# Results of seven items, added behind named steps of the eighth item's attention and experts

## The chip, the core and the metric

The kernel runs on one core of one Trainium2 chip, in one launch. The metric is device microseconds of that core. Three executions of the kernel before took 2759.94, 2760.19 and 2761.65 us; the median is 2760.19 us. The profiled execution of the same kernel took 2850.38 us, with a span of 2848.7 us from the first to the last instruction, so all times read from its trace are on a scale that is about 3% longer than the timed one.

## What is computed

The input is a batch of 8 items of 256 channels on a 32x32 grid, which is 1024 tokens of 256 features each, all in float32. An item passes two layers:

```python
# layer 0: 8 heads of 64, softmax over the queries' axis
qkv  = xt @ w_qkv + b_qkv
attn = softmax(einsum('bihd,bjhd->bijh', q, k) * SCALE, axis=1)
x    = einsum('bijh,bjhd->bihd', attn, v) @ w_out + b_out + xt
# layer 1: one attention without heads, then 8 experts of which each token uses 2
t = t + softmax((ln(t) @ W.T) @ ln(t).T) @ ln(t)
u = ln(t)
t = t + u + sum over the token's two best experts e of gate_e * (gelu(u @ w1[e] + b1[e]) @ w2[e] + b2[e])
```

Items don't depend on each other, except that the kernel treats the experts of seven of them together.

## The kernel before

**Stages.** A loop over the items b = 0 to 7 runs layer 0 (`layer0`) and, for the first seven, the attention of layer 1 (`attend`) and `dispatch`. The last function normalizes the tokens, finds each token's two experts and gates, and scatters the normalized rows into a DRAM tensor `rows`, one region for each expert, by 16 indirect DMAs on GpSimd's queue for an item (L631). It also keeps, for each item, the expert number `exp` and the row `row` of every token, and stores `sums` (the tokens plus their normalized form) in DRAM.

Item 7 is different. After its `layer0` comes `experts`, which handles the 7 x 1024 x 2 rows of the others in 63 blocks of 256 rows: for a block it fetches the weights of its expert and its rows by two indirect DMAs (L736, L745), transposes the rows (L754, copied out as `xb` on L756), multiplies twice (L764, L789), adds the bias on VectorE (L798, `yb`) and writes the result to the DRAM tensor `y` (L803). Then `attend` runs for item 7, and `dense`, in which every expert is applied to all 1024 tokens of item 7, in 16 steps of one expert and one half of the tokens (`hidden`, L938, and `collect`, L962 and L971).

**The plan.** `plan` turns the counts of rows for each expert into the numbers that the blocks need: `row_at` and `w_at` (which rows and which weights block b fetches), some 25 small VectorE instructions (L655 to L704), and then, for each of the seven items and both of a token's experts, `yat`, the place in `y` where the token's result lies: 14 times five instructions (L712 to L725), 70 in all.

**The others' results.** `Results` brings the results of the seven items together. It works in 14 portions, one for each half of an item. For a portion, `gather` issues 8 indirect DMAs on GpSimd's queue (L830), each of which fetches 128 rows of `y` into one eighth of a buffer `yk`; there are two such buffers, so two portions can be on their way. `step` takes one portion: if it is the first half of an item it loads `sums` into a buffer `o` (L852, SyncE's queue; two buffers, used in turn), then adds the 8 gathered pieces with their gates (L857, VectorE, eight instructions), lets the gather of the portion after next begin, and at the second half calls `store`: 16 transposes on TensorE (L877), two copies on ScalarE (L879) and two transfers to the output (L880).

**What sets the order.** The engines execute their own instructions in the order in which the scheduler of the language has put them. The scheduler lists instructions by the order in which the program makes them and by when it believes their inputs to be ready; it places instructions of one engine ahead of others when it expects a gap. The program says with `early` and `late` after which iterations of `attend` and of `dense` a portion is taken:

```python
        early = {3: 1, 4: 1, 5: 1, 6: 1, 7: 1}
        late = {0: 1, 1: 1, 2: 1, 4: 1, 5: 1, 7: 1, 8: 1, 10: 1, 12: 1}
```

Nothing keeps the scheduler from putting the additions of a portion ahead of that place. `tc.issue_after(instruction)`, which the kernel used before in `prepare`, does so: what the block under it makes on that instruction's engine is placed behind it. Instructions on other engines are not bound by it.

**Names along the way.** In `attend`, iteration i computes scores (L456, `ps`), their row maximum (VectorE, L464, `nmax`) and exponentials (ScalarE, L467, `ex`); `mix` then transposes them (L473, `pa`), copies them out (VectorE, L475, `aT`), multiplies by the tokens (L478, `py`) and adds the result (VectorE, L483). `mix` runs one iteration behind the scores. Before iteration 0 stand two copies of the projected tokens (VectorE, L448, `xa`). The PSUM pools have three buffers of two banks (`big`: scores, transposes, hidden layers, the output's transposes) and two of one bank (`acc`).

Of the kernel before, what the change touches and what calls it, by code (L numbers as in the profile page):

```python
# [18 lines left out]
def kernel(  # L19
# [23 lines left out]
    nc = tc.nc  # L43
    P = 128
    B, C, S = x.shape
# [6 lines left out]
    NH2 = S // 512  # L52
# [6 lines left out]
    NWB = 3  # L59
# [371 lines left out]
    def attend(b, t1, step=lambda i: None):  # L431
        n1 = one.tile([P, NT, D], F32, tag="n", name=f"n1_{b}")
        layer_norm(t1, n1, 1e-5, f"a{b}")
        nT = one.tile([P, NCC, S], F32, tag="nT", name=f"nT_{b}")
        to_channels(n1, nT, f"n1_{b}")
        xa = one.tile([P, NCC, S], F32, tag="xa", name=f"xa_{b}")
        for ec in range(NCC):
            px = big(f"px_{b}_{ec}")
            for dc in range(NCC):
                for n in range(NH2):  # L440
                    nc.tensor.matmul(
                        px[:, ts(n, 512)],
                        WT[:, dc, ts(ec, P)],
                        nT[:, dc, ts(n, 512)],
                        start=(dc == 0),
                        stop=(dc == NCC - 1),
                    )
            nc.vector.tensor_copy(xa[:, ec, :], px)  # L448

        t2 = t1  # L450

        def scores(i):
            psc = big(f"ps1_{b}_{i}")
            for ec in range(NCC):
                for n in range(NH2):
                    nc.tensor.matmul(  # L456
                        psc[:, ts(n, 512)],
                        xa[:, ec, ts(i, P)],
                        nT[:, ec, ts(n, 512)],
                        start=(ec == 0),  # L460
                        stop=(ec == NCC - 1),
                    )
            nmax = small.tile([P, 1], F32, tag="nmax", name=f"nmax_{b}_{i}")
            nc.vector.tensor_reduce(nmax, psc, AX.X, ALU.max, negate=True)  # L464
            ex = expp.tile([P, 1024], F32, tag="exps", name=f"ex1_{b}_{i}")
            ssum = small.tile([P, 1], F32, tag="ssum", name=f"ssum_{b}_{i}")
            nc.scalar.activation(ex, psc, AF.Exp, bias=nmax, scale=1.0, accum_out=ssum)  # L467
            return ex, ssum

        def mix(i, ex, ssum):  # L470
            pt = big(f"pa_{b}_{i}")
            for m in range(NT):
                nc.tensor.transpose(pt[:, ts(m, P)], ex[:, ts(m, P)], ident)  # L473
            aT = two.tile([P, S], F32, tag="tr", name=f"aT_{b}_{i}")
            nc.vector.tensor_copy(aT, pt)  # L475
            py = acc(f"py_{b}_{i}")
            for m in range(NT):
                nc.tensor.matmul(  # L478
                    py[:, :D], aT[:, ts(m, P)], n1[:, m, :], start=(m == 0), stop=(m == NT - 1)
                )  # L480
            rs = small.tile([P, 1], F32, tag="rs1", name=f"rs1_{b}_{i}")
            nc.vector.reciprocal(rs, ssum)
            nc.vector.scalar_tensor_tensor(  # L483
                t2[:, i, :], py[:, :D], rs, t1[:, i, :], ALU.mult, ALU.add
            )

        pending = None
        for i in range(NT):
            now = (i, *scores(i))
            if pending is not None:  # L490
                mix(*pending)
            pending = now
            step(i)
        mix(*pending)
        return t2

# [145 lines left out]
    def plan(group):  # L642


        n, nb, cap = group.n, group.nb, group.cap
        counts = group.counts
        steps = cap // BR
# [55 lines left out]
        w_at = keep.tile([P, NBMAX], I32, tag="w_at", name=f"w_at_{n}", bufs=2)  # L703
        nc.vector.tensor_copy(w_at[:, :nb], hi)  # L704


        for b in group.items:
            gate, kept = group.kept[b]
            ats = []
            for k, (row, exp) in enumerate(kept):  # L710
                hot = small.tile([P, NT, E], F32, tag="d_sel", name=f"p_hot_{b}_{k}", bufs=1)
                nc.vector.tensor_tensor(  # L712
                    hot,
                    exp.unsqueeze(2).to_broadcast([P, NT, E]),
                    e_iota.unsqueeze(1).to_broadcast([P, NT, E]),
                    ALU.is_equal,
                )
                nc.vector.tensor_mul(
                    hot, hot, first.unsqueeze(1).to_broadcast([P, NT, E])
                )  # L720
                to = small.tile([P, NT], F32, tag="d_to", name=f"p_to_{b}_{k}", bufs=2)
                nc.vector.tensor_reduce(to, hot, AX.X, ALU.add)
                nc.vector.scalar_tensor_tensor(to, to, float(BR), row, ALU.mult, ALU.add)
                at = keep.tile([P, NT], I32, tag=f"yat{k}", name=f"yat{k}_{b}")
                nc.vector.tensor_copy(at, to)  # L725
                ats.append(at)
            group.kept[b] = gate, ats
        return row_at, w_at

    def experts(group):  # L730
        n = group.n
# [51 lines left out]
        def collect(b, hT):  # L783
            wb = wbs[b % NWB]
            py = acc(f"pe_{n}_{b}")
            at = NCC * FF
            for r in range(R):
                for fc in range(NFC):
                    nc.tensor.matmul(  # L789
                        py[:, ts(r, D)],  # L790
                        hT[:, fc, ts(r, P)],
                        wb[:, at + fc * D : at + (fc + 1) * D],
                        start=(fc == 0),
                        stop=(fc == NFC - 1),
                    )
            at += NFC * D + NFC
            yb = two.tile([P, R, D], F32, tag="yb", name=f"yb_{n}_{b}")
            nc.vector.tensor_add(  # L798
                yb,
                py.rearrange("p (r d) -> p r d", d=D),  # L800
                wb[:, at : at + D].unsqueeze(1).to_broadcast([P, R, D]),
            )
            nc.sync.dma_start(group.y[ts(b, BR), :].rearrange("(p r) d -> p r d", r=R), yb)  # L803

        line = [None, None]
        for b in range(group.nb + 2):
# [77 lines left out]
    def dense(b, t2, step):  # L884
# [71 lines left out]
        def collect(e, n, hT):  # L956
            wb = wbs[e % NWB]
            for i in range(0, NT // NH2, 2):
                py = acc(f"pdy_{e}_{n}_{i}")
                for j in range(2):  # L960
                    for fc in range(NFC):
                        nc.tensor.matmul(  # L962
                            py[:, ts(j, D)],
                            hT[:, fc, ts(i + j, P)],
                            wb[:, NCC * FF + fc * D : NCC * FF + (fc + 1) * D],
                            start=(fc == 0),
                            stop=(fc == NFC - 1),
                        )
                for j in range(2):
                    block = n * (NT // NH2) + i + j  # L970
                    nc.vector.scalar_tensor_tensor(  # L971
                        t2[:, block, :],
                        py[:, ts(j, D)],
                        all_gates[:, block, e : e + 1],
                        t2[:, block, :],
                        ALU.mult,
                        ALU.add,
                    )
            if n == NH2 - 1 and e + NWB < E:
                weights(e + NWB)  # L980
            if e == E - 1:
                store(b, t2, range(n * (NT // NH2), (n + 1) * (NT // NH2)))

        pending = None
        for at, (e, n) in enumerate((e, n) for e in range(E) for n in range(NH2)):
            now = (e, n, hidden(e, n))
            if at == 1:
                biases()
            if pending is not None:
                collect(*pending)  # L990
            pending = now
            step(at)
        collect(*pending)

    for b in range(B):
        xT = next_x
        if b + 1 < B:
            next_x = load_x(b + 1)
        t1 = layer0(b, xT)
        if b + 1 < B:  # L1000
            t2 = attend(b, t1)
            dispatch(b, t2, groups[0])
            continue
        experts(groups[0])
        others = Results(groups[0])
        others.begin()

        early = {3: 1, 4: 1, 5: 1, 6: 1, 7: 1}
        late = {0: 1, 1: 1, 2: 1, 4: 1, 5: 1, 7: 1, 8: 1, 10: 1, 12: 1}

        def step(where, at):
            for _ in range(where.get(at, 0)):
                others.step()

        t2 = attend(b, t1, lambda i: step(early, i))
        dense(b, t2, lambda i: step(late, i))
        assert others.done == len(others.portions)
# [42 lines left out]
```

## Time and profile before

| | |
|---|---|
| timed, median of 3 | 2760.19 us |
| profiled execution, span | 2848.7 us |
| TensorE busy | 2656.4 us, 93% of the span |
| VectorE busy | 1540.0 us, 54% |
| ScalarE busy | 841.6 us, 30% |
| GpSimd busy | 384.9 us, 14% |
| mean granted TensorE clock | 0.964 |
| additions of the others' results (L857) | 112 x 479 ns (median) |
| gathers of results (L830) | 112 x 953 ns (median) |
| attention and experts of item 7 | 2543 to 2849 us of the span |

TensorE sets the pace over most of the span: in the layer 0 of an item it is busy without pause. Idle time on the other engines costs nothing there. It is different at the end, from 2543 us on, where the table of engines by stage (in the prediction below) shows TensorE idle for a third of the attention of item 7. The duration of an L830 row is [...]not the time until the rows have landed. The name in brackets behind an instruction of the timeline is what ended its engine's idle time before it; "issue" and "remote" mean that the profile shows no wait of the program that would explain it.

### The profile page before, as it was taken

The numbers are of one execution on the slowest core, as the hardware profiler recorded it, in microseconds if no ns is written. First come the engines' busy times: TensorE is split into PE (matmuls) and PEld (weight loads), VectorE is DVE, ScalarE is ACT, GpSimd is POOL, SyncE is SP. The second block draws the span as 40 slices with busy tenths as digits, with TensorE's granted clock in tenths as the row PEclk, the third lists the DMA queues.
The fourth block names the chain that finished last, engine by engine and source line by source line (L and its number), as shares of the span: only waits on it lengthen the run. The fifth ranks groups of instructions, "written<-read, shape, count | busy, mean of one in ns | idle before, by whom it ended". The sixth has DMA issues, their size and how long they took to land. (4 is left out here: it accounts for less than half of the span.)

```text
span 2848.7 us, 27710 instructions
## 1 busy us (share of the span) xinstructions
PE 2656.4 (93%) x10153; PEld 1401.7 (49%) x10153; DVE 1540.0 (54%) x3667; ACT 841.6 (30%) x1455; POOL 384.9 (14%) x383
## 2 busy tenths in 40 slices
PE   8999899989998999999999999999989999986789
PEld 3346434643365336533553356335633577764556
DVE  4664566456645674467456755565476633333442
ACT  2541154114511451045214521342125411111122
POOL 0000200020002000100011000200030044445540
PEclk9999999999999999999999999999989999997789
DMA  6981100010001000000000000000020155542351
GB/s 243 385 316 25 59 1 1 15 45 1 1 15 43 3 1 15 30 15 1 15 21 24 1 15 15 30 1 1 15 69 1 37 178 177 177 151 81 108 173 56
DMA packets 82512, 182.37 MB, mean 64 GB/s; under 512 B 15016, under 2 KB 24904, under 8 KB 80584
## 3 DMA queue, kind: packets, MB, share of 16 engines
q1 hardware_dynamic: 57368, 118.65, 11.6%
q0 software_dynamic: 25008, 61.95, 6.8%
q8 instruction: 80, 1.31, 0.2%
q14 instruction: 56, 0.46, 0.0%
HBM read 100.49 MB, written 110.90 MB: 74 GB/s over the span
## 5 line engine op out<-in xcount | busy, mean ns | idle before, releaser
L357 ACT ACTIVATE ex<-psc,nmax 128x1024 f32<-128x1024 f32 x512 | 565.8, 1109 | 827.6 <-DVE scrap L347 636.7
L324 PE MATMUL psc<-qk,qk 64*128 64x512 f32 x2048 | 590.7, 625 | 33.1 <-ACT ex L357 17.1
L382 PE MATMUL po<-ex,vs 128*64 128x512 f32 x2048 | 506.4, 616 | 8.1 <-DVE vs L366 7.1
L335 DVE TENSOR_REDUCE nmax<-psc 128x1 f32<-128x512 f32 x512 | 351.4, 687 | 169.4 <-PE psc L324 160.4
L324 PEld LDWEIGHTS psc<-qk,qk 64*128 64x128 f32 x2048 | 232.1, 186 | 385.7 <-ACT ex L357 187.3
L347 DVE TENSOR_SCALAR_CACHE_REDUCE scrap<-psc,nmax 128x512 f32<-128x512 f32 x512 | 382.2, 746 | 54.3 <-PE psc L324 22.5
L382 PEld LDWEIGHTS po<-ex,vs 128*64 128x64 f32 x2048 | 126.4, 137 | 352.6 <-issue 193.5
L478 PE MATMUL py<-n,aT 128*128 128x256 f32 x1024 | 243.3, 392 | 41.4 <-issue 21.9
L638 POOL TENSOR_TENSOR t<-t,n 128x2048 f32<-128x2048 f32 x7 | 31.6, 4512 | 1793.5 <-issue 1503.9
L456 PE MATMUL ps<-nT,xa 128*128 128x512 f32 x512 | 240.7, 600 | 10.6 <-DVE xa L448 5.7
L478 PEld LDWEIGHTS py<-n,aT 128*128 128x128 f32 x1024 | 195.6, 195 | 99.9 <-DVE aT L475 51.6
L273 PE MATMUL pqk<-xT,wqkv 128*128 128x512 f32 x512 | 238.7, 612 | 2.4 <-ACT ex L357 2.0
L281 DVE TENSOR_SCALAR qk<-pqk,b_qk 128x1024 f32<-128x1024 f32 x64 | 82.1, 1284 | 189.9 <-PE pqk L273 188.0
L467 ACT ACTIVATE ex<-ps,nmax 128x1024 f32<-128x1024 f32 x64 | 71.3, 1114 | 382.5 <-DVE nmax L464 359.8
L273 PEld LDWEIGHTS pqk<-xT,wqkv 128*128 128x128 f32 x512 | 95.7, 195 | 150.4 <-issue 104.7
L483 DVE SCALAR_TENSOR_TENSOR t<-py,rs,t 128x256 f32<-128x256 f32 x64 | 31.0, 484 | 242.8 <-PE py L478 215.5
L292 PE MATMUL pv<-wqkv,xT 128*128 128x512 f32 x256 | 138.5, 691 | 9.1 <-ACT wqkv L97 7.3
L456 PEld LDWEIGHTS ps<-nT,xa 128*128 128x128 f32 x512 | 94.7, 193 | 92.1 <-issue 79.9
L789 PE MATMUL pe<-wb,hb 128*128 128x256 f32 x504 | 125.5, 392 | 10.9 <-ACT hb L774 7.9
L631 POOL DMA_INDIRECT rows<-n,d_at x112 | 108.9, 973 | 158.6 <-DVE row L618 106.8
L830 POOL DMA_INDIRECT yk<-y,yat x112 | 111.9, 999 | 120.6 <-DVE o L857 71.5
L420 PE MATMUL pr<-wo,res 128*128 128x256 f32 x512 | 122.0, 381 | 0.0
(171 smaller groups left out, 2500.9 us busy)
## 6 DMA issues: line engine op xcount, KB each, us to landing
rows<-wb SPq DMA_DIRECT2D x7, 8192.0 KB
y<-yb SPq DMA_DIRECT2D x63, 256.0 KB
xT<-in_x_dram SPq DMA_DIRECT2D x7, 1024.0 KB
sums<-t SPq DMA_DIRECT2D x7, 1024.0 KB
o<-sums SPq DMA_DIRECT2D x7, 1024.0 KB
out_dram<-oT SPq DMA_DIRECT2D x14, 512.0 KB
wpack<-in_L_ffn_w_dram SPq DMA_DIRECT2D x4, 1024.0 KB
wb<-in_L_ffn_w_dram SPq DMA_DIRECT2D x16, 256.0 KB
```

What stands on the lines that cost most here:

```text
L273: nc.tensor.matmul(pq[:, ts(n, 512)], wqkv[:, cc, t, ts(g, P)], xT[:, cc, ts(n, 512)], start=(cc == 0), stop=(cc == NCC - 1),)
L292: nc.tensor.matmul(pv[:, ts(j, 512)], xT[:, cc, ts(i + j, P)], wqkv[:, cc, 2, :], start=(cc == 0), stop=(cc == NCC - 1),)
L324: mm = nc.tensor.matmul(pss[at, h][:, ts(n, 512)], k[r, ts(j, P)], q[r, ts(n, 512)], start=True, stop=True)
L335: firsts[at, h] = nc.vector.tensor_reduce(nmax, pss[at, h][:, ts(0, 512)], AX.X, ALU.max, negate=True)
L347: nc.vector.tensor_scalar(scrap, ps[:, ts(1, 512)], -1.0, nmaxes.pop((at, h)), ALU.mult, ALU.min, accum_out=nmax,)
L357: nc.scalar.activation(ex, ps, AF.Exp, bias=nmax, scale=1.0, accum_out=sums[at][:, h : h + 1])
L382: nc.tensor.matmul(po[n][h * DK : (h + 1) * DK, :], vs[:, h, :], exs[h][:, ts(n, 512)], start=(j == 0), stop=(j == NT - 1),)
L420: nc.tensor.matmul(pr[:, :C], res[:, g, ts(i, P)], wo[:, g, :], start=(g == 0), stop=False)
L456: nc.tensor.matmul(psc[:, ts(n, 512)], xa[:, ec, ts(i, P)], nT[:, ec, ts(n, 512)], start=(ec == 0), stop=(ec == NCC - 1),)
L478: nc.tensor.matmul(py[:, :D], aT[:, ts(m, P)], n1[:, m, :], start=(m == 0), stop=(m == NT - 1))
L789: nc.tensor.matmul(py[:, ts(r, D)], hT[:, fc, ts(r, P)], wb[:, at + fc * D : at + (fc + 1) * D], start=(fc == 0), stop=(fc == NFC - 1),)
L830: nc.gpsimd.indirect_dma_start(out=yk[:, i, k, :], out_offset=None, in_=self.group.y[:, :], in_offset=bass.IndirectOffsetOnAxis(ap=ats[k][ ...
```

## The change

Four edits, all of them in the order of instructions; the work is the same.

- The portions are bound to named instructions. In `attend`, `step(i)` moves from the loop into `mix`, behind the addition of iteration i (L483). In `dense`, it moves into `collect`, behind the last addition of that step (L971). The additions of a portion can no longer stand ahead of these on VectorE.
- `early` and `late` are set anew: six portions in the attention instead of five, two at once behind the first step of `dense`.
- The plan of the blocks is bound to the last copy of q and k of item 7's layer 0 (`evicted[7, 3, 1]`, L281), where before it could stand as soon as the counts were known.
- The places of results (`yat`) are taken out of the plan into a function `places`, bound to the bias addition of expert block 3 (L798).

Line numbers below are those of the kernel before; in the changed kernel the same lines stand 1 to 13 lines further down.

```diff
-            nc.vector.scalar_tensor_tensor(
+            mixed = nc.vector.scalar_tensor_tensor(
                 t2[:, i, :], py[:, :D], rs, t1[:, i, :], ALU.mult, ALU.add
             )
+            with tc.issue_after(mixed.ins):
+                step(i)
 ...
             pending = now
-            step(i)
         mix(*pending)
 ...
     def plan(group):
+        with tc.issue_after(evicted[B - 1, NPAIR - 1, 1].ins):
+            return plan_blocks(group)
+
+    def plan_blocks(group):
 ...
-
+        group.first = first
+        return row_at, w_at
+
+    def places(group):
+
+        first = group.first
         for b in group.items:
 ...
             group.kept[b] = gate, ats
-        return row_at, w_at
 ...
             nc.sync.dma_start(group.y[ts(b, BR), :].rearrange("(p r) d -> p r d", r=R), yb)
+            if b == NWB:
+                with tc.issue_after(added.ins):
+                    places(group)
 ...
+            with tc.issue_after(added.ins):
+                step(e * NH2 + n)
             if n == NH2 - 1 and e + NWB < E:
                 weights(e + NWB)
 ...
             pending = now
-            step(at)
         collect(*pending)
 ...
-        early = {3: 1, 4: 1, 5: 1, 6: 1, 7: 1}
-        late = {0: 1, 1: 1, 2: 1, 4: 1, 5: 1, 7: 1, 8: 1, 10: 1, 12: 1}
+        early = {1: 1, 2: 1, 3: 1, 5: 1, 6: 1, 7: 1}
+        late = {0: 2, 3: 1, 4: 1, 6: 1, 8: 1, 9: 1, 11: 1}
```

## The prediction, made before the changed kernel ran

> **What bounds the kernel now.** I read the page first: TensorE is busy 93% of the span and every other engine at most 54%, so other engines matter only where TensorE waits for them. The slices of the page show two such places: the end (from 2543 us), and a dip near 2100 us. Then I asked for the stages. The columns are: stretch and its length, busy us (and instructions) of PE, PEld, DVE, ACT and POOL, granted TensorE clock, DMA share, GB/s.
>
> ```profile
> 2543.20:2683.00 139.80, 89.53 (x329) 58.25 (x327) 60.32 (x121) 17.83 (x26) 76.08 (x78) 0.84 0.36 110
> ...
> 2690.00:2849.00 159.00, 144.28 (x536) 98.16 (x535) 54.51 (x141) 34.31 (x49) 33.92 (x33) 0.90 0.31 103
> ...
> 1206.79:1242.28 35.49, 31.69 (x96) 11.20 (x96) 19.77 (x46) 12.81 (x22) 9.94 (x11) 0.95 0.12 41
> 1787.38:1825.76 38.38, 33.09 (x96) 11.51 (x96) 19.75 (x46) 12.81 (x22) 9.92 (x11) 0.91 0.11 38
> 2083.92:2130.33 46.41, 35.96 (x97) 12.40 (x96) 29.23 (x117) 12.81 (x22) 16.64 (x17) 0.82 0.27 94
> ```
>
> The first two are item 7's attention and its experts. TensorE is idle for 50.3 of 139.8 us in the attention, and the clock falls to 0.84. The last three are the same work (from the first q and k of an item to those of its second pair of heads) at the start of items 4, 6 and 7: 35.5 us usually, 46.4 us in item 7, where VectorE has 9.5 us more to do, the plan.
>
> Then the timeline of item 7's attention, VectorE first:
>
> ```profile
> 2551.63 1.23 DVE L448 COPY xa<-px 128x1024 f32<-128x1024 f32 x1 [2.66 <-PE px L441]
> 2553.13 0.49 DVE L857 SCALAR_TENSOR_TENSOR o<-yk,gate,o 128x256 f32<-128x256 f32 x1 [0.27 <-DMA yk<-y,yat]
> ...
> 2560.73 0.48 DVE L857 SCALAR_TENSOR_TENSOR o<-yk,gate,o 128x256 f32<-128x256 f32 x1 [2.10 <-DMA yk<-y,yat]
> 2561.13 1.22 DVE L448 COPY xa<-px 128x1024 f32<-128x1024 f32 x1
> ...
> 2582.56 1.23 DVE L475 COPY aT<-pa 128x1024 f32<-128x1024 f32 x1 [4.65 <-remote]
> ...
> 2606.43 0.48 DVE L483 SCALAR_TENSOR_TENSOR t<-py,rs,t 128x256 f32<-128x256 f32 x1 [17.08 <-remote]
> ...
> 2668.60 0.48 DVE L483 SCALAR_TENSOR_TENSOR t<-py,rs,t 128x256 f32<-128x256 f32 x1 [5.99 <-remote]
> ```
>
> and what TensorE makes of it:
>
> ```profile
> 2562.40 8.36 PE L456 MATMUL ps<-nT,xa 128*128 128x512 f32 x12 [5.66 <-DVE xa L448]
> ...
> 2583.84 6.17 PE L478 MATMUL py<-n,aT 128*128 128x256 f32 x16 [10.49 <-issue]
> ...
> 2610.74 6.37 PE L478 MATMUL py<-n,aT 128*128 128x256 f32 x16 [9.69 <-DVE aT L475]
> ...
> 2620.42 3.72 PE L478 MATMUL py<-n,aT 128*128 128x256 f32 x16
> ```
>
> The second `xa` copy has its input at 2555.0 but stands behind five additions (L857), which wait for gathers, so it starts at 2561.1 and TensorE loses 5.66 us. The same happens to `aT` of iterations 0 and 1. Each pause also costs clock: the same 16 records take 6.2 to 6.4 us after one and 3.72 us without. In the experts the chain of waits names another wait, the load of `sums`, issued too late on SyncE's queue:
>
> ```profile
> 2706.12 6.44 DMA o<-sums
> ...
> 2738.89 5.97 DMA o<-sums
> ...
> 2759.28 6.55 DMA o<-sums
> ```
>
> At full clock the attention needs 74.6 us of TensorE: 2.0 + 7.1 (first transposes, projection), 8 x (3.44 + 0.87 + 3.45), two items' output transposes at 1.75. So 65 us are lost, 50 idle and 15 to the clock.
>
> **What I can't read.** The rows marked "remote" (4.65, 17.08, 5.99, and 3.35 before another `aT`; in the experts 1.34 and 4.97) are waits whose release the trace doesn't show. The inputs were there by the trace, and GpSimd had been issuing gathers without pause. The profiled execution is 90 us longer than the timed one (2850.38 against 2760.19). I take these pauses to belong to the profiled execution. Taking them out shifts the attention by 15 us at `aT` of iteration 1 and 12 us at the end, 27 together, and the experts by 8.7 (6.7 and 2 of clock). That leaves, as an estimate for the timed run, 113 us for the attention and 150 for the experts.
>
> **What the Trainium skill says.** "TensorE: Matmul & The Clock Gate", section "What's actually happening": after an idle window of about 3.4 us the array runs at half clock until it has been busy for about as long. The trace agrees (6.17 against 3.72 us above). "DMA: Bandwidth & Descriptors", section on one DMA on the gpsimd path: about 2.0 us plus bytes over 436 GB/s, 2.3 us for a gather of 128 KB. Here the first gather was issued at 2550.32 and its addition began at 2553.13, 2.8 us, the issue included. [...] "SBUF — State Buffer", section "Who interferes with whom": an operation with two SBUF inputs disturbs only GpSimd operations that read SBUF. The gathers keep their pace of 1.26 us (0.95 + 0.30) beside the additions, so I price that interference at nothing.
>
> **The change, part by part.**
>
> *Attention.* It takes away every addition ahead of `xa`, `nmax` and `aT` of iterations 0 and 1, and puts 8 (0.40 us start to start, 3.3 us) behind L483 of iterations 1, 2, 3, 5, 6, 7. Queued behind them are the next `nmax` and `aT`; ScalarE waits for the first, TensorE for both. Walking through with the durations above: `xa` ready at 2556.3, scores 0 and 1 done at 2561.6, `aT` 0 at 2564.3, `py` 0 done at 2567.9, `py` 1 at 2575.7. Then the additions show: the output's transposes stand on TensorE ahead of `py` 2 and wait for the first portion (1.3 us), `py` 2 waits for `aT` 2 (1.8 us), `aT` 7 stands behind the additions of iteration 6 (about 4.5 us), and small waits for PSUM buffers. I get L483 of iteration 7 at 2635.6. The last portion (3.3 us) lies on the path to the normalization: its transposes then start at 2640.8. Before, they start at 2683.05, without the unread pauses at 2656. Gain **15 us**. Are the gathers there in time? A portion is 8 x 1.26 = 10.1 us of GpSimd. Portions 0 and 1 end at 2570; portion 2 starts when the first is consumed (2579.5) and is needed at 2598.6; portion 3 is there at 2602, needed at 2614; 4 at 2614, needed at 2627; 5 at 2630, needed at 2636. Yes.
>
> *Experts.* The loads of `sums` now stand ahead of the item's output in SyncE's queue, and their buffers are free 20 us or more before use; so the three waits above go, and with them TensorE pauses of 1.9 and 2.4 us and about 3.5 us of clock behind the first. One portion less is left (0.9 us of transposes). Against this, the transposes of a portion wait in order for its additions, about 1.5 us at the two portions behind step 0. Gain **5 us**.
>
> *Start of item 7.* Plan and places leave 2075 to 2121 us. Of 46.41 - 35.48 = 10.9 us, item 6 shows 2.9 without any plan; of the other 8 about 2 go with a "remote" 2.70 us. Gain **6 us**.
>
> *Plan late in layer 0.* Its 25 instructions make about 6.6 us, spread over five steps of 3.9 us in which VectorE waits 0.6 to 1.0 us for TensorE. Five steps give about 4 us, the rest is exposed: **cost 3 us** (0 if the lag of two steps hides it, 6.6 if nothing does). It ends near 2230; the first block begins at 2272, so its fetches (1 us of issue each) are hidden.
>
> *Places among the expert blocks.* 70 instructions of about 0.17 us, 12 us, over eight half blocks with 1.47 us of idle VectorE each, 11.8 us. `xb` is needed 1.3 us after it is made, so the small overhang is hidden: **0** (4 at most).
>
> Sum: 15 + 5 + 6 - 3 - 0 = 23 us, 2760 - 23 = **2737 us**.
>
> **The rivals.**
> - *The unread pauses are in the timed run too* (20%). Then the old attention loses all 65 us. The new one has no more than 16 gathers in a row where the old had 40; if two thirds of 36 us go as well, 24 more: 2713. For it: the pauses come with long rows of gathers. Against: TensorE pauses too, without a wait of its own, and the total is long by 90 us in the profile.
> - *Smaller* (15%). In-order transposes and PSUM buffers (three, of which two now hold an output) eat the attention's gain down to 8, the start gives 5, the plan costs 3: 2750.
> - *Nothing* (7%): 8 more us lost in the same places, 2758.
> - *Slower* (6%). Every portion in the attention costs its 3.3 us and clock on top (30 of the 38 us that I think are lost now, a gain of 8), the eight in the experts cost 1.5 us each (-12, +7), plan 6.6 and places 6 are exposed, and the start gives 2: 2760 + 8 = 2768. Against it: four of the six are beside scores.
>
> **Numbers.** My case has 52%. The range is 2712 to 2754: below it lies half of the first rival, above it the last two. Faster by over 0.2% (below 2754.7): 0.52 + 0.20 + 0.15 = 0.87; within: 0.07; slower: 0.06.
>
> **What would show it.** In the profile of the changed kernel: both `xa` copies side by side and the first scores before 2560; no L857 wait on `sums`; attention near 98 us instead of 139.8; the start of item 7 at 36 to 40 us; the late part of layer 0 longer by up to 3 us; expert blocks still 4.33 us apart. I am wrong if TensorE's pauses only move: if it waits for the output's transposes behind additions in most iterations, if the plan stops layer 0 for more than 6 us, or if the gap between profiled and timed run stays at 90 us, which would mean that the pauses weren't the profiler's.

## The result: 12.7 us less, and the profile after

The changed kernel takes 2747.36 us (median of four executions, 2742.55 to 2748.91), the kernel before 2760.07 in the same comparison. The ratio is 0.9954, with a 95% interval of 0.9936 to 0.9972. The forecast was 23 us, 0.9917.

Not every run had the same chip: the kernel before takes 2759 to 2760 us beside this result and the runs e1 to e4, but 2857 to 2860 us on the three chips of e5 to e12, so a time is to be compared only with the kernel before beside it. I call them the first and the second kind of chip.

The profiled execution of before that the prediction reads took 2850.38 us, and fits the second kind. Its times aren't the timed ones on a longer scale: against e1 it is 45 us longer ahead of item 7's attention, 29 us in it and 16 us behind. Its stages are therefore no measure of the 12.7 us. I profiled the kernel before once more (e1, span 2758.1 us), and use that one here. The page of the changed kernel, and that of e1:

```profile
span 2745.2 us, 27697 instructions
...
PE 2617.9 (95%) x10153; PEld 1378.9 (50%) x10153; DVE 1539.6 (56%) x3667; ACT 841.2 (31%) x1455; POOL 385.7 (14%) x383
```

```profile
span 2758.1 us, 27710 instructions
...
PE 2620.8 (95%) x10153; PEld 1380.4 (50%) x10153; DVE 1544.5 (56%) x3667; ACT 842.3 (31%) x1455; POOL 386.8 (14%) x383
```

The work is the same; TensorE waits less. The engines by stage show where (columns as in the prediction). Kernel before, e1: attention of item 7, its experts, the start of item 7, the late part of its layer 0 (from its last q and k to the end of its output products):

```profile
2497.85:2608.80 110.95, 85.42 (x330) 56.20 (x328) 60.58 (x121) 18.09 (x26) 68.02 (x69) 0.92 0.43 130
2608.80:2758.10 149.30, 142.82 (x552) 96.41 (x552) 63.41 (x149) 34.62 (x50) 49.08 (x44) 0.93 0.38 120
2051.14:2084.95 33.81, 29.64 (x97) 10.51 (x96) 28.81 (x117) 12.82 (x22) 16.86 (x17) 1.00 0.38 129
2163.97:2226.66 62.69, 62.36 (x277) 30.72 (x277) 41.08 (x107) 27.64 (x47) 0.95 (x1) 1.00 0.06 22
```

Changed kernel, the same four stretches:

```profile
2496.84:2600.84 104.00, 87.86 (x346) 57.44 (x344) 52.70 (x105) 19.64 (x28) 57.42 (x60) 0.93 0.42 131
2600.84:2745.20 144.36, 138.16 (x536) 92.75 (x536) 64.82 (x165) 32.58 (x48) 59.68 (x54) 0.95 0.39 129
2051.03:2081.86 30.83, 29.00 (x96) 10.53 (x96) 19.76 (x46) 12.81 (x22) 9.94 (x11) 1.00 0.14 47
2160.86:2225.72 64.86, 62.56 (x276) 30.84 (x277) 45.73 (x127) 27.62 (x47) 6.95 (x7) 1.00 0.19 63
```

Attention -7.0 us, experts -4.9, start -3.0, plan +2.2: together -12.7 us. The 63 expert blocks take 270.9 us in both (first L764 or L773 to the attention's first transposes). VectorE's own load shows the moved plan: 28.81 to 19.76 us in the start, 41.08 to 45.73 in the late part.

The front of the attention is where the change does most. Kernel before, e1: VectorE's timeline, then TensorE's:

```profile
2506.27 1.22 DVE L448 COPY xa<-px 128x1024 f32<-128x1024 f32 x1 [2.66 <-PE px L441]
2507.84 0.48 DVE L857 SCALAR_TENSOR_TENSOR o<-yk,gate,o 128x256 f32<-128x256 f32 x1 [0.35 <-DMA yk<-y,yat]
2510.42 0.88 DVE L857 SCALAR_TENSOR_TENSOR o<-yk,gate,o 128x256 f32<-128x256 f32 x2 [2.09 <-DMA yk<-y,yat]
...
2515.81 1.22 DVE L448 COPY xa<-px 128x1024 f32<-128x1024 f32 x1
```

```profile
2517.09 8.03 PE L456 MATMUL ps<-nT,xa 128*128 128x512 f32 x12 [5.70 <-DVE xa L448]
...
2533.87 6.45 PE L478 MATMUL py<-n,aT 128*128 128x256 f32 x16 [6.17 <-DVE aT L475]
...
2550.08 5.19 PE L478 MATMUL py<-n,aT 128*128 128x256 f32 x16 [4.59 <-DVE aT L475]
```

Changed kernel, the same two engines:

```profile
2505.26 1.22 DVE L448 COPY xa<-px 128x1024 f32<-128x1024 f32 x1 [2.66 <-PE px L441]
2508.70 1.22 DVE L448 COPY xa<-px 128x1024 f32<-128x1024 f32 x1 [2.21 <-PE px L441]
```

```profile
2508.49 7.03 PE L456 MATMUL ps<-nT,xa 128*128 128x512 f32 x16
...
2518.03 3.72 PE L478 MATMUL py<-n,aT 128*128 128x256 f32 x16
...
2525.92 3.72 PE L478 MATMUL py<-n,aT 128*128 128x256 f32 x16
```

The additions between the two `xa` copies waited for gathers, one or two at a time; behind the change the copies follow TensorE at once. The `py` of iteration 1 begins 52.2 us after the attention's first transposes before (2550.08 - 2497.85) and 29.1 us after the change (2525.92 - 2496.84): 23.1 us won. From there to the normalization it is 58.7 us before and 74.9 after: 16.2 us given back. Net 7.0 us.

Why so much is given back shows when the additions are counted. By `early` the kernel before has five portions in the attention, but its trace has 64 additions there, eight portions: the scheduler drew them forward. The changed kernel has 48, six portions as written, and so two portions more than before in the experts. The first four of the eight stand at the front and cost the 23.1 us. Of the 32 additions of the other four, 29 stand between a copy `aT` and the next L483, where VectorE waits for TensorE anyway (e1, VectorE):

```profile
2575.73 1.21 DVE L475 COPY aT<-pa 128x1024 f32<-128x1024 f32 x1
...
2577.54 3.63 DVE L857 SCALAR_TENSOR_TENSOR o<-yk,gate,o 128x256 f32<-128x256 f32 x9
2581.10 0.47 DVE L483 SCALAR_TENSOR_TENSOR t<-py,rs,t 128x256 f32<-128x256 f32 x1
```

Item 6, which has no portions, takes 51.7 us from the `py` of iteration 1 to its normalization (2021.21 - 1969.47, changed kernel). Beside that the four late portions of the kernel before cost 7.0 us, 1.7 us each, and the six of the changed kernel, behind L483, 23.2 us, 3.9 us each; both sums include the transposes of the output, of two and of three items. So the change takes additions away from the worst place, but puts those that stood well in a worse one.

### The profile page after: what moved, and what is told of

Same layout as the page of the kernel before. It is cut to its first block, busy times and chain, and to the rows that moved or that the text cites. A ratio compares the mean times of both kernels' runs of the same rounds, so it can differ in the third digit from the quotient of the medians.

```text
span 2745.2 us, 27697 instructions
## 1 busy us (share of the span) xinstructions
PE 2617.9 (95%) x10153; PEld 1378.9 (50%) x10153; DVE 1539.6 (56%) x3667; ACT 841.2 (31%) x1455; POOL 385.7 (14%) x383
## 4 chain that ended last, share of the span: by engine, by line
PE 83%; issue 8%; DVE 4%; ACT 3%; DMA 0%; POOL 0%; ACTq 0%; SPq 0%; DVEq 0%
PE psc L324 20%; PE po L382 17%; PE pqk L273 8%; PE py L478 8%; PE ps L456 7%; PE pv L292 5%; PE pr L420 4%; PE px L441 2%; PE pdh L950 2%; PE pdy L974 2%; PE pt_n L218 2%; PE pa L473 2%; PE pe L798 1%; PE pl L504 1%; ACT hb L783 1%
## 5 line engine op out<-in xcount | busy, mean ns | idle before, releaser
L324 PE MATMUL psc<-qk,qk 64*128 64x512 f32 x2048 | 581.0, 624 | 16.8 <-DVE qk L281 11.0
L382 PE MATMUL po<-ex,vs 128*64 128x512 f32 x2048 | 495.9, 605 | 6.6 <-DVE vs L366 6.6
L478 PE MATMUL py<-n,aT 128*128 128x256 f32 x1024 | 241.5, 390 | 10.9 <-DVE aT L475 10.9
L281 DVE TENSOR_SCALAR qk<-pqk,b_qk 128x1024 f32<-128x1024 f32 x64 | 82.2, 1284 | 186.7 <-PE pqk L273 186.7
L483 DVE SCALAR_TENSOR_TENSOR t<-py,rs,t 128x256 f32<-128x256 f32 x64 | 31.0, 484 | 230.9 <-PE py L478 230.9
L798 PE MATMUL pe<-wb,hb 128*128 128x256 f32 x504 | 125.4, 392 | 10.9 <-ACT hb L783 10.8
L842 POOL DMA_INDIRECT yk<-y,yat x112 | 112.6, 1005 | 98.5 <-DVE o L869 52.2
```

Of the source, the lines that this page charges most:

```text
L324: mm = nc.tensor.matmul(pss[at, h][:, ts(n, 512)], k[r, ts(j, P)], q[r, ts(n, 512)], start=True, stop=True)
L382: nc.tensor.matmul(po[n][h * DK : (h + 1) * DK, :], vs[:, h, :], exs[h][:, ts(n, 512)], start=(j == 0), stop=(j == NT - 1),)
L478: nc.tensor.matmul(py[:, :D], aT[:, ts(m, P)], n1[:, m, :], start=(m == 0), stop=(m == NT - 1))
L798: nc.tensor.matmul(py[:, ts(r, D)], hT[:, fc, ts(r, P)], wb[:, at + fc * D : at + (fc + 1) * D], start=(fc == 0), stop=(fc == NFC - 1),)
L842: nc.gpsimd.indirect_dma_start(out=yk[:, i, k, :], out_offset=None, in_=self.group.y[:, :], in_offset=bass.IndirectOffsetOnAxis(ap=ats[k][ ...
```

## The experiments

**e1: the kernel before, profiled again.** No edit.

> The kernel before, unchanged, profiled once more. Theory A (the forecast's: the unread pauses and the 90 us between profile and timed run belong to that one profiled execution): the span is near 2758 us, no unread pause above 3 us, attention of item 7 (first transposes to the normalization's transposes) near 113 us instead of 139.8, its experts near 157 us up to the end instead of 166, start of item 7 about 44 us instead of 46.4. Rival B (the pauses come with this order of instructions, wherever it is profiled): the profile is again some 90 us longer than the timed run, and rows of 4 to 17 us without a visible release stand again in item 7's attention.

Measured: span 2758.1 us, 2760.14 us timed (0.9997 to 1.0018 of before). No wait in this trace is put down to "remote", where the first profile had 64 us of them. Attention 110.95 us (theory A: 113), start 33.8 (44 expected). On this kind of chip the pauses aren't there. They aren't those of a single execution either: here all 37 executions of the kernel before took 2752 to 2765 us, and in the comparisons of e5 to e12 all 37 took 2842 to 2866. So the long times, and the pauses that their profiles show, go with the chip, or with something else that differed between these sessions, each of which had its own chip.

**e2: the portions alone**, with the new places; plan and places of results as before.

```diff
-        with tc.issue_after(evicted[B - 1, NPAIR - 1, 1].ins):
-            return plan_blocks(group)
 ...
-            if b == NWB:
-                with tc.issue_after(added.ins):
-                    places(group)
```

> The first two edits alone: portions bound to named steps, with the new places; plan and places as before. Theory A with the sizes that the changed kernel's profile suggests (attention 104 us rather than the 97.6 forecast): 9 us of the attention and 5 of the experts, 14 in all, so 2746 us, the same as the whole change, since plan and places nearly cancel. Rival C (the steps bring the forecast 20 us and plan and places cost 7 of it): 2740 us. Rival D (most of the gain comes from the start of item 7): 2753 us or more.

Measured: 2747.47 us, ratio 0.9958 (0.9945 to 0.9971), attention 103.5 us. This is the whole of the change's gain, as theory A (2746) had it; C (2740) and D (2753) miss.

**e3: plan and places of results alone.**

```diff
-            with tc.issue_after(mixed.ins):
-                step(i)
 ...
-            with tc.issue_after(added.ins):
-                step(e * NH2 + n)
 ...
+        early = {3: 1, 4: 1, 5: 1, 6: 1, 7: 1}
+        late = {0: 1, 1: 1, 2: 1, 4: 1, 5: 1, 7: 1, 8: 1, 10: 1, 12: 1}
```

> The last two edits alone: plan late in layer 0, places among the expert blocks; portions as before. Theory A: start of item 7 gains 6 by the forecast, plan costs 3: 2757 us, at most 2760. Rival C: the exposed plan costs more than the start brings, 2767 us. Rival D: 2750 us.

Measured: 2755.89 us, ratio 0.9990 (0.9981 to 0.9999). By the stages: start 33.81 to 30.83 us, late part 2.2 us longer, blocks unchanged, so -0.8; attention 111.3 us, again with eight portions in it. It neither costs much (C) nor carries the gain (D).

**e4: bound, but with the old places of the portions.**

```diff
-        early = {1: 1, 2: 1, 3: 1, 5: 1, 6: 1, 7: 1}
-        late = {0: 2, 3: 1, 4: 1, 6: 1, 8: 1, 9: 1, 11: 1}
+        early = {3: 1, 4: 1, 5: 1, 6: 1, 7: 1}
+        late = {0: 1, 1: 1, 2: 1, 4: 1, 5: 1, 7: 1, 8: 1, 10: 1, 12: 1}
```

> The portions bound to the named steps but with the old places (five in the attention behind iterations 3 to 7, nine in the experts); plan and places as before. If binding is what pays (additions leave the front of xa and aT, loads of sums go early): within 3 us of the kernel with both edits, so 2743 to 2749. If the new places matter as much: half of that gain, 2753. If five portions in a row behind iterations 3 to 7 each cost their 3.3 us: 2760 or more.

Measured: 2743.95 us, ratio 0.9943 (0.9929 to 0.9956); attention 99.8 us. Binding is what pays: bound, the portions are where the program puts them. The new places take some of it back: beside e2, on the same chip, the old ones are 3.5 us faster by the medians, and each of the six executions of e4 (2738.97 to 2744.26) is faster than each of the six of e2 (2744.40 to 2748.64). The attention has one portion less than that of e2 and is 3.7 us shorter, and the nine portions left for the experts don't lengthen these (143.9 us to the end, 147.3 in e2). Whether eight portions, bound behind L483, would be slower than the kernel before was not run.

The remaining runs were meant to find what the attention still loses, and fell on the other kind of chip.

**e5 and e10: additions behind the copy `aT`**, not behind L483. In the changed kernel VectorE idles 3.5 to 5.4 us between `aT` and L483 in seven of the eight iterations, long enough for a portion's additions (3.25 us).

```diff
-            nc.vector.tensor_copy(aT, pt)
+            copied = nc.vector.tensor_copy(aT, pt)
 ...
-            with tc.issue_after(mixed.ins):
+            with tc.issue_after(copied.ins):
                 step(i)
```

> The changed kernel with one edit: the portions of the attention are bound to the copy aT of their iteration instead of to the addition L483 that follows it one product later. Theory E (what is left of the attention's loss is VectorE's order: the additions stand ahead of the next nmax and aT, while VectorE idles for 3.5 to 5.1 us behind each aT): the additions fall into that idle time; attention near 90 us instead of 104 (81.4 us in item 6, without portions, plus six times 0.87 us of transposes, plus the last portion's some 3 us), so 2747 - 14 = 2733 us. Rival F (TensorE's in-order transposes of the output and their PSUM buffers cost the time, wherever the additions stand): within 4 us of the changed kernel, 2743 to 2751 us.

> The changed kernel with the portions of the attention bound to the copy aT of their iteration. Theory E: additions in VectorE's idle time, attention near 90 us, 2733 us (or 14 us below the changed kernel). Rival F: transposes of the output in TensorE's order cost the time: within 4 us of the changed kernel.

Measured: e5 2829.18 beside 2860.41 us (0.9883, 0.9855 to 0.9911), e10 2828.96 beside 2856.63 (0.9892, 0.9867 to 0.9918). The changed kernel, beside e10, has 2822.75, not told apart from it by six executions each (2810 to 2835 and 2814 to 2833). Theory E's 14 us don't come, and rival F's number, no change, fits. Timeline of e10, ScalarE and VectorE:

```profile
2603.59 1.01 ACT L891 COPY oT<-pout 128x1024 f32<-128x1024 f32 x1 [4.65 <-remote]
...
2661.77 0.48 DVE L483 SCALAR_TENSOR_TENSOR t<-py,rs,t 128x256 f32<-128x256 f32 x1 [13.94 <-remote]
2661.95 1.93 ACT L891 COPY oT<-pout 128x1024 f32<-128x1024 f32 x2 [26.81 <-remote]
```

But the pauses overlap rows of 16 and 24 gathers (2583 to 2603 us and 2628 to 2659), in which TensorE idles 5.6 and 13.4 us. They hide the gain of the order, if there is one, so these runs don't decide between E and F.

**e6 and e7: four early portions; the whole change with the old places.**

```diff
 # e6
+        early = {1: 1, 2: 1, 4: 1, 5: 1}
+        late = {0: 1, 1: 1, 2: 1, 4: 1, 5: 1, 7: 1, 8: 1, 9: 1, 10: 1, 12: 1}
 # e7
+        early = {3: 1, 4: 1, 5: 1, 6: 1, 7: 1}
+        late = {0: 1, 1: 1, 2: 1, 4: 1, 5: 1, 7: 1, 8: 1, 10: 1, 12: 1}
```

> The changed kernel with four portions in the attention (behind iterations 1, 2, 4, 5, none behind 6 and 7) and ten in the experts. The undisturbed attention of item 6 has 81.4 us without portions, the changed one 104.0 with six: 3.8 us a portion. Theory E: the two portions at the end cost more than the mean, because the normalization waits for them and for ScalarE's copies of the output; attention 94 us, experts plus 2 us for two more portions: 2739 us. Rival F: 2 x 0.87 us of transposes only move: 2746 us.

> The changed kernel with the old places of the portions (early 3 to 7, late as before). By the stages of the runs so far: attention 99.8 and experts 139.4 us as with binding alone, start and plan 0.9 us better than that kernel: 2743 us. If the places of results among the expert blocks hinder the gathers: 2747 us or more.

Measured: 2829.32 us (0.9902, 0.9876 to 0.9928) and 2831.75 (0.9919, 0.9889 to 0.9949). Neither is told from the changed kernel's 0.9894 (e9). The attention takes 105.3 and 105.8 us (e9: 112.0), the experts 170.0 and 179.6 to the end (e9: 166.7): they shift the loss. The absolute times expected don't apply to this chip.

**e8: no additions in the attention.**

```diff
-            for i in range(NT // 2):
+            for i in range(NT // 2 if at >= 6 else 0):
                 block = half * (NT // 2) + i
```

> The changed kernel without the additions of the six portions in the attention (48 instructions are left out; gathers, loads of sums, output transposes, copies and transfers stay). Theory E: VectorE's additions are the loss: attention 81.4 + 5.2 = 87 us, at most 90. Rival F: transposes and PSUM buffers are the loss: 97 us or more.

Measured: 2869.60 us in its one execution, and an attention of 151.7 us: with 48 instructions less it is the slowest of all, slower than all eleven executions of the kernel before beside it (at most 2866.38). Its timeline, VectorE and TensorE:

```profile
2606.16 0.48 DVE L483 SCALAR_TENSOR_TENSOR t<-py,rs,t 128x256 f32<-128x256 f32 x1 [35.27 <-remote]
...
2617.39 1.23 DVE L464 TENSOR_REDUCE nmax<-ps 128x1 f32<-128x1024 f32 x1 [10.06 <-remote]
2639.84 1.22 DVE L475 COPY aT<-pa 128x1024 f32<-128x1024 f32 x1 [21.23 <-remote]
```

```profile
2641.12 4.12 PE L478 MATMUL py<-n,aT 128*128 128x256 f32 x11 [62.22 <-DVE aT L475]
```

Nothing consumed the gathers, so GpSimd issued 64 in one row, from 2556 to 2636 us, one every 1.26 us. In that row TensorE idled 58 us. VectorE waited with its input there: the `py` before L483 had ended at 2574.6. So the pauses need no additions; what they lie over is the row of gathers. Between theory E and rival F the run says nothing. The floor of the attention that this run was meant to give comes from item 6, which has no portions (profile of the changed kernel):

```profile
1939.83:2021.21 81.38, 75.27 (x288) 48.36 (x289) 36.69 (x63) 13.22 (x20) 0.00 (x0) 0.98 0.00 0
```

**e9: the changed kernel on such a chip.** No edit.

> The changed kernel once more, beside the next two kernels on one chip. On a chip where the kernel before takes 2760 us: 2747 us, attention 104 us. On the chip of the last four runs, where the kernel before took 2860 us: with the theory that rows of gathers stop the engines there (G), the change, which lets no more than 16 gathers run in a row before the first additions, gains more than on the other chip, near 2831 us; with the theory that this chip only stretches everything (H): 0.9954 of 2860, 2847 us.

Measured: 2822.75 beside 2856.63 us, 0.9894 (0.9864 to 0.9924): 33.9 us, where the other chip gave 12.7. Theory H (2847) falls. Theory G's number (2831) is passed. Here the change gains about 21 us more. The profiles fit that: from the first one of before to that of e9 the attention becomes 27.8 us shorter (139.8 to 112.0), the experts 1 us longer.

**e11: behind the copies, five early portions.**

```diff
 # on e10
+        early = {1: 1, 2: 1, 3: 1, 4: 1, 5: 1}
+        late = {0: 1, 1: 1, 2: 1, 4: 1, 5: 1, 7: 1, 8: 1, 10: 1, 12: 1}
```

> The same, with five portions behind the copies of iterations 1 to 5 and none behind 6 and 7, and the places in the experts of before. Theory E: one portion less (0.87 us moved) and nothing between the last product and the normalization but what item 6 has: attention near 86 us, experts 139 to 141: 2729 us. Rival F: attention 98 us or more as in the kernel with the old places, 2743 us.

Measured: 2842.05 us, 0.9945 (0.9920 to 0.9970), 19 us slower by the medians than the changed kernel on that chip. Portions in five iterations on end let the gathers run in rows of 16, 16 and 16, with some 5.5 us of idle TensorE each in the second and third; and 141 us of waits of all engines are put down to "remote", against 53 in e9.

**e12: behind the copies of iterations 1, 3 and 5 only.**

```diff
 # on e10
+        early = {1: 1, 3: 1, 5: 1}
+        late = {0: 1, 1: 1, 3: 1, 4: 1, 5: 1, 7: 1, 8: 1, 9: 1, 11: 1, 12: 1, 13: 1}
```

> The changed kernel with the portions of the attention behind the copies aT of iterations 1, 3 and 5 only, and eleven in the experts. Theory E (additions in VectorE's idle time behind aT, nothing behind the last product): on a chip where the kernel before takes 2760 us, attention 81.4 + 3 x 0.87 + some 2 us, about 86 us, experts 142.5, so some 15 us below the changed kernel, 2732 us or 0.990 of before. Rival F (output transposes and PSUM buffers): attention 95 us, 2744 us. On the chip of the last runs (before 2857 us), theory G (rows of gathers stop the engines; here portions are two iterations apart, so no row in the attention is longer than 16 and most are 8): attention at most 95 us instead of 112 to 120, experts as before, 2806 us; theory H (no relation to rows): pauses of 20 us or more in the attention as in the kernel with six portions behind the copies.

Measured: 2810.05 beside 2856.57 us, 0.9855 (0.9828 to 0.9881), the best ratio of all runs on this kind of chip; attention 92.4 us (G: at most 95). H falls: the one pause of the attention stands behind its one row of 16 gathers, and none beside its three rows of eight. The interval still touches that of e9, which had another chip, so as a whole it is probably, not surely, faster than the change. The last gather of the row of 16, and VectorE's timeline from there:

```profile
2556.89 0.96 POOL L842 DMA_INDIRECT yk<-y,yat  x1 [0.31 <-issue]
...
2560.82 0.48 DVE L483 SCALAR_TENSOR_TENSOR t<-py,rs,t 128x256 f32<-128x256 f32 x1 [8.70 <-remote]
...
2569.70 0.48 DVE L483 SCALAR_TENSOR_TENSOR t<-py,rs,t 128x256 f32<-128x256 f32 x1 [2.24 <-PE py L478]
2572.55 1.21 DVE L475 COPY aT<-pa 128x1024 f32<-128x1024 f32 x1
2577.64 0.48 DVE L483 SCALAR_TENSOR_TENSOR t<-py,rs,t 128x256 f32<-128x256 f32 x1 [3.57 <-PE py L478]
2580.44 1.21 DVE L475 COPY aT<-pa 128x1024 f32<-128x1024 f32 x1
2581.57 3.25 DVE L869 SCALAR_TENSOR_TENSOR o<-yk,gate,o 128x256 f32<-128x256 f32 x8
2585.64 0.48 DVE L483 SCALAR_TENSOR_TENSOR t<-py,rs,t 128x256 f32<-128x256 f32 x1 [0.75 <-PE py L478]
```

From L483 to L483 it is 7.94 us without a portion and 8.00 us with one: behind `aT` the additions stand beside `py`, and what was an idle of 3.57 us is one of 0.75. That is theory E, shown for the additions of this portion; the iteration behind it takes 10.9 us, with 11 of the item's 16 output transposes in it. The third portion stands in an iteration of 7.8 us, followed by one of 8.1: it costs nothing that shows. The pause costs TensorE 4.1 us of idle time and 1.7 us of clock; without it, by this estimate, the attention would take 86.6 us, as theory E had it for a chip of the first kind (about 86), where the kernel was not run. Three portions instead of six and their spacing were changed together, so how much each brings is open.

## Why the prediction was right, and where it was off

**The bound and the mechanism at the front: right.** TensorE's waits at the front of the attention were additions standing ahead of `xa`, `nmax` and `aT`; both `xa` copies now keep TensorE's pace, and the 16 first score products run in one piece from 11.7 us behind the first transposes (2508.49 - 2496.84), where I had named 16.8 as the latest (2560 - 2543.2). That sign was set too wide: in e1 too the first four start after 11.7 us, and it is the other twelve that wait, until 19.2 (2517.09 - 2497.85). e2 shows that binding the portions carries the gain, e4 that it does so with the old places.

**The count of portions: wrong.** I took the places in the program for those in the trace: five portions before, six after, so one less for the experts. The trace that I read has 64 additions in the attention, eight portions. The change leaves the additions of two portions more to the experts (and 16 transposes less, those of one item), and of the additions that I moved behind L483 half had stood well.

**"What I can't read": half right.** I took the unread pauses to belong to one profiled execution. On the chip of the result they are absent, as assumed (e1: 110.95 us of attention against my estimate of 113, though from the router on the experts took 145.5, 2758.10 - 2612.64, instead of 150). But they don't belong to one execution. On the second kind of chip they come in every profile, the times there are as long in every execution, and the first rival comes near: it gave the change 24 us more, e9 shows 21 more. That the result fell on a chip without them is luck. The rival's sign, the pauses coming with long rows of gathers, was right, and e8 shows it at its barest. What it doesn't cover: 45 of the 90 us lie ahead of the attention, where no results are gathered.

**Attention, 15 us: 7.0.** This is the term that was mis-sized, 2 us on the side of before and 6.4 on that of after (104.0 instead of 97.6). My walk was right to the `py` of iteration 1 within 0.3 us. Then two things are missing. It gave every `py` 3.72 us, but three behind a wait for the output's transposes or `aT` each ran into 3.4 us of half clock, which the clock records have from 2535.9, 2576.8 and 2587.1 us on (TensorE, changed kernel):

```profile
2535.95 5.27 PE L478 MATMUL py<-n,aT 128*128 128x256 f32 x16
...
2576.72 5.41 PE L478 MATMUL py<-n,aT 128*128 128x256 f32 x16
2587.00 5.41 PE L478 MATMUL py<-n,aT 128*128 128x256 f32 x16 [0.69 <-DVE aT L475]
```

That is 4.9 us (1.55 + 1.69 + 1.69), against the 3.2 us by which L483 of iteration 7 came late: I had charged the clock to the old pauses and nothing to the new ones. (In e2, with the same order in the attention, the same three take 6.50, 3.72 and 5.20 us, so what each one loses varies.) And the last portion costs more than its additions (VectorE, then ScalarE):

```profile
2592.45 0.48 DVE L483 SCALAR_TENSOR_TENSOR t<-py,rs,t 128x256 f32<-128x256 f32 x1 [4.95 <-PE py L478]
2592.85 3.25 DVE L869 SCALAR_TENSOR_TENSOR o<-yk,gate,o 128x256 f32<-128x256 f32 x8
...
2596.68 0.17 DVE L205 TENSOR_SCALAR rstd_f<-mv_f 128x8 f32<-128x8 f32 x1
2600.04 0.20 DVE L207 RECIPROCAL rstd_f<-rstd_f 128x8 f32<-128x8 f32 x1 [3.19 <-ACT rstd_f L206]
```

```profile
2596.56 1.93 ACT L891 COPY oT<-pout 128x1024 f32<-128x1024 f32 x2 [20.28 <-PE pout L889]
2598.51 1.28 ACT L206 ACT_TABLE_LOAD   x1
2599.80 0.21 ACT L206 ACTIVATE rstd_f<-rstd_f 128x8 f32<-128x8 f32 x1
```

The item's output is copied by ScalarE, in order ahead of the root that the normalization waits for: the two copies hold L206 from 2596.85 (L205's end) to 2598.51, and the table that L206 needs is loaded only then, another 1.28 us. From the end of the last `py` (2592.41) to the transposes (2600.84) there are 8.4 us; in item 6, without a portion, 2.48. So the last portion costs 6.0 us on the path; I had allowed 5.2 us from L483 to the transposes in all, and there are 8.4. e4 has the counterpart: its last portion is an item's first half, which has no output to copy, L207 waits 0.27 us for L206 instead of 3.19, and there are 5.5 us.

**Experts, 5 us: 4.9, but partly chance.** In the undisturbed profile the kernel before waits for `sums` as I said (its chain of waits; the first of the two is still in the attention):

```profile
2589.82 6.41 DMA o<-sums
...
2625.98 6.40 DMA o<-sums
```

Behind the change no instruction of the tail waits for it, nor in e2 and e4. But up to the last matmul the two profiles with the old order have 144.9 (e1) and 142.4 us (e3), the three with bound portions 139.9, 142.9 (e2) and 139.4 us (e4). Profiles of one order differ by 3 us, and e2 shows no gain over e3. By the means it is about 3 us, with two or three portions more to handle; that the waits went is shown, what they were worth is not.

**Start of item 7, 6 us: 3.0.** The direction was right; the size was read from the profile with the pauses. In e1 the start costs only 2.98 us more than that of item 6 (30.83), and the change takes away all of it.

**Plan, 3 us: 2.2. Places of results, 0: 0.** VectorE has 4.65 us more to do in the late part (I had 6.6) and 2.2 are exposed. The blocks keep their 270.9 us.

Of the rivals, "nothing" and "slower" fell with the result. "Smaller" is nearer to it (2750) than my own number, though its sum leaves the experts' gain out: it had 8 us for the attention, and one of its reasons, transposes in TensorE's order that wait, stands ahead of the slow `py` whose clock I left out.

## What to carry to other kernels

Work that fills gaps should stand behind the last instruction that the critical engine waits for, and ahead of the next idle time: here behind `aT`, where VectorE waits for TensorE anyway, not behind L483, where the next `nmax` and `aT` are due. The traces of e1 and e12 show this for single portions; no timed run on a chip without pauses does. Where filler work stands is read from the trace and not from the program, in which eight portions looked like five. What takes the place of a removed wait costs clock as well, so a forecast charges it to both sides; and behind a last portion one asks for every engine on the path what it still has to do for that portion. Sizes are read only from a profile whose span fits the time to be explained; here one that was 3% above it showed the mechanism at the front, but not its worth.

## What was new about the hardware

- On some chips long rows of gathers on GpSimd's queue go with pauses of 3 to 35 us on VectorE and ScalarE, without any wait in the trace that would explain them; on another chip there are none (48 gathers in a row in e1, where VectorE waits for the gathers' data only). The length of the row tells them apart: in the nine profiles of the second kind 38 of 41 rows of 16 or more gathers have such a pause of over 2.5 us in them or within 4 us behind them, and one of 26 rows of eight, which follows another row by 1 us. Many of the pauses end with the row: in the seven runs whose attention begins with 16 gathers in a row (e5 to e7, e9 to e12) L483 of iteration 0 starts 2.85 to 2.97 us behind the end of the last of them, after waiting 8.0 to 8.7 us. What the engines wait for is open, and so is what makes the items ahead of the attention longer on these chips: item 6 takes 290 to 297 us against 286.7, with at most 2.6 us of such pauses.
- Short pauses are enough to lose clock, and when they do is a matter of phase. Two items of e1, the same program (items 3 and 4 from one first q and k to the next):

```profile
900.87:1187.54 286.67, 275.27 (x1044) 132.28 (x1044) 170.42 (x410) 93.38 (x159) 20.18 (x18) 0.99 0.04 15
1187.54:1477.64 290.10, 278.60 (x1045) 134.58 (x1044) 170.52 (x410) 93.38 (x159) 20.21 (x18) 0.98 0.04 15
```

Both have the same pauses of TensorE, of at most 2.5 us, but by the clock records the first has 6.8 us at half clock and the second 13.6, in stretches of 3.4 us or multiples, and the difference of 3.4 us is what the second is longer. The Trainium skill ("TensorE: Matmul & The Clock Gate", section "What's actually happening") says that the window of 3413 ns, over which the activity is watched, runs freely and doesn't begin anew with a kernel; the stretches in this trace begin on such a grid (those at 583.60 and 211.55 us are 109 steps of 3.413 us apart). The idle window of about 3.4 us that the prediction names isn't needed: here no pause is that long, and the measurement decides. A few such steps more or less in eight items are of the size of the spread between executions, 2751.9 to 2764.4 us for the kernel before; that they cause it isn't shown.
